# Splitting the gates' biases in the first layer, and running the last feed by halves of its tokens

## The chip, the core and the metric

The kernel runs on one core of a Trainium2 chip, in one launch. The time is the device time of an execution in microseconds. Measured times come from several executions; the profile comes from one execution of its own.

## What is computed

The reference is a chain of twelve blocks on 16 batches of 64 tokens with 256 features (1024 tokens), each added to its input after a layer norm. The change lies in four of them, one after the other:

```python
x = x + L0_xattn(layernorm(x), ctx_1024, ...)   # cross-attention, 16 heads, to 1601 context rows a batch
x = x + L0_attn(layernorm(x), ...)              # four encoder layers of linear attention, feed of 1024
x = x + L0_ffn(layernorm(x), ...)               # 8 experts, 2 for a token
x = x + L1_xattn(layernorm(x), ctx_1024, ...)   # slots: three rounds of attention and a GRU

# an encoder layer of L0_attn ends with
h = _layernorm(x, ln2_s, ln2_b)
h = jax.nn.relu(h @ W1 + b1) @ W2 + b2
return x + h
# the routing of L0_ffn
logits = x @ gate_w.T
top2_w, top2_idx = jax.lax.top_k(softmax(logits), 2)
counts = bincount(top2_idx); keep = counts <= cap
# the gates of L1_xattn
gx = x @ wih.T + bih
gh = h @ whh.T + bhh
r = sigmoid(xr + hr); z = sigmoid(xz + hz); n = tanh(xn + r * hn)
```

## The kernel before

A `Sections` object writes one method per block. `self.x` holds all tokens in on-chip memory as 8 tiles of 128 tokens (two batches each). The framework orders the instructions of each engine by their place in the program and by when it expects them to be ready, except where the code pins them (`keep_in_program_order`, the wrapper `Written`, the helpers `mm` and `tr`). So a load stands early in SP's queue when its memory is free, and blocks the loads behind it while it waits.

**First layer (`l0_xattn`).** `stream` walks the 16 batches' context in pairs of chunks. `load(b)` issues the two DMAs of batch b's transposed context `cT`; `maxima`, `weights`, `values` and `finish` work on one large score tile of PSUM ("w", one buffer). VectorE reduces maxima, ScalarE takes the exponential, POOL sums the weights into `tot` (tag "tot", two buffers). Products are pinned once the prologue is over, VectorE's instructions are not.

**Linear attention (`l0_attn`).** The tokens are in two halves `a` and `b` of 512, each with two pairs p of tiles. Small generators (`project`, `attend`, `feed`, `route`) yield between groups of instructions, and `go(it, n)` advances one by n steps, so that the order of all engines in this block is written by hand. `feed` turns the normed tokens, makes eight chunks c of 128 features of `relu(h @ W1 + b1)` over all 512 tokens (`by_feature`, 512 columns, evacuated by ScalarE for even c and by VectorE for odd), then four products with W2 (`by_token`, t) that VectorE adds to `y`; `measure` and `norm` are the two halves of a layer norm, `finish` the last one of the block. `squares` puts pieces of the slots' context norms on ScalarE in between. `route(s, p)` chooses the two experts of a pair's 256 tokens: turn, product with the gate (`gate`), a sort on VectorE (`rk_gt`, `rk_eq`, `rank`, `sel`), counts, the product `pos` (place of each token within its expert), the places on VectorE, and four indirect DMAs by POOL that scatter rows into the DRAM buffer `taken`. Counts run on from pair to pair, so routes come in order. The buffers of the routes lie in the pool "l0r", opened at the head of `l0_attn`; the rest is in pools on the right side of memory. PSUM's tag "mm" (chunks, `gate`, `pos`) has three buffers.

In the last layer, `a` ends first. Its two pairs are routed between the chunks of `b`'s feed, `b`'s two pairs after that feed.

**Experts (`l0_ffn`).** `xs` is read from `taken` once all scatters have landed, two products per expert follow, and results go to the DRAM buffer `given`.

**Slots (`l1_xattn`).** `load_keys` loads `cT` for the two batches of a tile (four DMAs of 832 KB), `load_rows` their rows `cn`. `product` multiplies weight matrices (`pw`). `biases` adds the two GRU biases, splits the sum in three BF16 parts on rows 24 to 26 of `bias`, which one product with `three` adds to the gates. `fetch(t)` gathers the experts' rows into `got`, `combine(t)` adds them to `self.x`, and from that `first` makes tile t's slots. `attend` (scores, turn, exponential) and `update` (`pu`, gates) follow by turns for two tiles at a time.

Of the kernel before, what the change touches and what calls it, by code (L numbers as in the profile page):

```python
# [64 lines left out]
class Sections:  # L65
# [135 lines left out]
    def l0_xattn(self):  # L201
        nc, tc, d = self.nc, self.tc, self.d
        with ExitStack() as ctx:
# [31 lines left out]
            def load(b):  # L235
                x = Streamed(b)
# [172 lines left out]
    def l0_attn(self):  # L409
# [3 lines left out]
        self.routed = ExitStack()  # L413
        pool = self.routed.enter_context(tc.tile_pool(name="l0r", bufs=1, reuse_waits="tile"))
        self.routes = to = Streamed(0)
# [18 lines left out]
        with ExitStack() as ctx:  # L434
# [260 lines left out]

            def route(s, p):
# [27 lines left out]
                V.tensor_tensor(to.count[:, 2 * g + 1], to.count[:, 2 * g], sel[:, 0], ALU.add)  # L724
                pos = ps.tile([P, 2, E], F32, tag="mm", name="pos", bufs=3, padded_shape=[P, 64, E])
# [89 lines left out]
            fb = feed(b, w, True)  # L815
# [3 lines left out]
            for p in range(2):  # L819
                measure(a, a.x, p)  # L820
                rt = route(a, p)
                go(fb, 1)
                norm(a, a.x, p)
                for _ in range(3):
                    go(rt, 1)
                    go(fb, 1)

            go(fb, 2)
            measure(b, b.x, 0)
            go(fb, 1)  # L830
            r0, r1 = route(b, 0), route(b, 1)
            norm(b, b.x, 0)
            go(r0, 1)
# [3 lines left out]
            go(r0, 1)  # L837
            go(r1, 1)
            go(r0)
            go(r1)  # L840
# [125 lines left out]

    def l1_xattn(self):
# [3 lines left out]
        with ExitStack() as ctx:  # L971
# [47 lines left out]

            at = ROWS_AT["L1_xattn_gru_bih"][0], ROWS_AT["L1_xattn_gru_bhh"][0]  # L1020
            raw, raw2 = (sb2.tile([32, 4 * D], F32, tag="e", name="raw", padded_shape=[32, NCH * P]) for _ in range(2))
            nc.gpsimd.memset(raw, 0.0)
            nc.gpsimd.memset(raw2, 0.0)
            for t, to, of, n in ((raw, 0, at[0], G), (raw, G, at[1] + 2 * D, D), (raw2, 0, at[1], 2 * D)):
                nc.sync.dma_start(t[24:27, to : to + n], d["rows"][:, of : of + n].to_broadcast([3, n]))
# [15 lines left out]

            bias = sb.tile([P, 4 * D], BF16, tag="bias", name="bias")
            three = sb.tile([P, P], BF16, tag="three", name="three")

            def biases():

                third = self.c("third")
# [1745 lines left out]
```

## Time and profile before

| | us |
|---|---|
| measured, 3 executions: median (lowest to highest) | 3773.07 (3768.23 to 3774.36) |
| the profiled execution: its time | 3775.53 |
| its span, first to last instruction | 3773.7 |
| first layer, to its last product | 0 to 863.9 |
| linear attention, to the landing of the last scatter | to 1356.5 |
| experts, to their last product | to 1383.7 |
| slots | to about 1930 |

The mean granted clock of TensorE is 0.957 of full speed. PE is TensorE, PEld its weight loads, DVE VectorE, ACT ScalarE, POOL GpSimd, SP SyncE; "q" behind an engine is its queue. A timeline line gives start, duration, engine, source line, operation, output<-input with shapes, a count, and in brackets how long the engine was idle before it and what ended the wait. L59 and L2429 are the lines of helpers, so groups are told apart by the names of tiles. A line by windows gives start:end and length, the busy time of PE, PEld, DVE, ACT and POOL with the number of instructions, then TensorE's granted clock, the busy share of the DMA engines and GB/s.

### The profile page before, as it was taken

What the parts mean: (1) busy time and instruction counts of PE and PEld (TensorE: products, weight loads), DVE (VectorE), ACT (ScalarE), POOL (GpSimd) and SP (SyncE); (2) the same over time, 40 slices, a digit from 0 to 9 for tenths busy, and PEclk for the clock granted to TensorE, in tenths of its full rate; (3) what the DMA queues carried; (4) which work ended last, traced back from release to release, by engine and by line L of the source; (5) the groups of instructions that cost most, each with busy time, mean ns of one, the idle gap of its engine ahead of it and who ended that gap; (6) DMA issues with size and microseconds to landing.
All of it is one profiled execution on the core that took longest, in us unless ns stands there. A gap on an engine that the chain in (4) does not pass through costs nothing.

```text
span 3773.7 us, 70724 instructions
## 1 busy us (share of the span) xinstructions
PE 3435.9 (91%) x30919; PEld 2176.2 (58%) x30934; DVE 1972.4 (52%) x3672; ACT 1450.6 (38%) x2072; POOL 1291.7 (34%) x789
## 2 busy tenths in 40 slices
PE   8999999996999858999977988999999789999986
PEld 4555555563666544555544666667767555555454
DVE  4344333345555546656656545576767655333346
ACT  2333333342444413444423443466666612111214
POOL 1555555561101132333321001577777630000012
PEclk9999999998999978999988999999999979999997
DMA  3111101101333352442101000211111004111650
GB/s 126 38 38 38 38 20 38 38 10 58 104 97 97 110 180 102 145 146 105 42 26 40 1 6 28 83 56 38 54 40 38 11 2 173 39 37 32 256 199 13
DMA packets 106046, 258.42 MB, mean 68 GB/s; under 512 B 9181, under 2 KB 74464, under 8 KB 103433
## 3 DMA queue, kind: packets, MB, share of 16 engines
q1 hardware_dynamic: 97288, 222.43, 16.6%
q10 hardware_dynamic: 6912, 27.27, 2.3%
q8 instruction: 243, 3.98, 0.4%
q0 software_dynamic: 1536, 4.20, 0.4%
q14 instruction: 67, 0.54, 0.0%
HBM read 248.10 MB, written 5.77 MB: 67 GB/s over the span
## 4 chain that ended last, share of the span: by engine, by line
PE 77%; DVE 12%; ACT 7%; issue 3%; POOL 0%; DMA 0%; ACTq 0%; SPq 0%; DVEq 0%; POOLq 0%
PE sc L2429 15%; PE pk L2429 15%; PE lin L2429 7%; PE acc L2429 6%; PE lin_t L2429 5%; ACT e L322 4%; PE pu L2429 4%; PE lin L194 3%; PE gate L1994 3%; PE up L1994 3%; PE pc L1616 3%; PE prz L2429 2%; PE gelu_t L1526 2%; PE turn L2434 2%; PE pn L2429 1%
## 5 line engine op out<-in xcount | busy, mean ns | idle before, releaser
L2362 POOL TENSOR_TENSOR tot<-tot,e 128x1024 f32<-128x1024 f32 (+1 forms) x340 | 803.3, 2363 | 374.6 <-ACT e L322 251.9
L265 DVE TENSOR_REDUCE m<-sc 128x4 f32<-128x2048 f32 x96 | 220.1, 2293 | 273.1 <-PE sc L2429 272.1
L1756 DVE SCALAR_TENSOR_TENSOR e<-sc,row_L_xattn_nbias,free 128x2048 f32<-128x2048 f32 x104 | 244.3, 2349 | 122.6 <-PE sc L2429 118.8
L1758 ACT ACTIVATE e<-e 128x2048 f32<-128x2048 f32 x104 | 198.7, 1910 | 243.0 <-DVE e L1756 243.0
L322 ACT ACTIVATE e<-sc 128x2048 f32<-128x2048 f32 x104 | 195.2, 1877 | 242.8 <-PE sc L2429 238.7
L2429 PE MATMUL sc<-qb,kT 32*128 32x128 f32 x6656 | 245.9, 284 | 36.3 <-DVE m L279 12.4
L2429 PEld LDWEIGHTS sc<-qb,kT 32*128 32x128 f32 x6656 | 207.0, 187 | 80.4 <-issue 24.5
L2429 PE MATMUL acc<-e,v 128*32 128x128 f32 x6656 | 226.3, 276 | 6.4 <-ACT e L1759 6.4
L2429 PEld LDWEIGHTS acc<-e,v 128*32 128x32 f32 x6656 | 170.0, 110 | 105.8 <-issue 95.2
L2429 PE MATMUL pk<-cT,wk 128*128 128x512 f32 (+1 forms) x512 | 207.5, 534 | 3.6 <-DVE rows L295 3.6
L2429 PE MATMUL pk<-wv,cT 128*128 128x256 f32 x832 | 208.6, 393 | 0.0
L1759 ACT ACTIVATE e<-e 128x2048 f32<-128x2048 f32 x104 | 198.7, 1911 | 3.3
L2429 PE MATMUL pk<-cT,wkv 128*128 128x512 f32 (+1 forms) x512 | 196.4, 524 | 0.0
L2429 PE MATMUL pk<-wkv,cT 128*128 128x256 f32 x832 | 196.3, 386 | 0.0
L2429 PEld LDWEIGHTS pk<-wv,cT 128*128 128x128 f32 x832 | 149.3, 189 | 75.2 <-issue 57.2
L2429 PEld LDWEIGHTS pk<-wkv,cT 128*128 128x128 f32 x832 | 153.2, 190 | 28.4 <-issue 4.3
L2429 PE MATMUL pu<-cn,e 128*64 128x257 f32 (+1 forms) x1248 | 146.6, 392 | 12.9 <-POOL e L1162 12.9
L1616 PE MATMUL pc<-ew,eh 128*128 128x256 f32 x640 | 155.0, 384 | 0.0
L1998 ACT ACTIVATE g<-gate 128x512 f32<-128x512 f32 x68 | 40.6, 597 | 292.2 <-PE gate L1994 292.2
L2429 PE MATMUL sc<-kT,qb 32*128 32x512 f32 (+2 forms) x1536 | 139.6, 463 | 11.4 <-ACT e L322 0.4
L1152 POOL TENSOR_TENSOR e<-e,mx 128x512 f32<-128x512 f32 x96 | 81.8, 884 | 195.2 <-DVE mx L1151 190.8
L2429 PE MATMUL sc<-cT,qT 128*64 128x512 f32 (+1 forms) x768 | 140.3, 518 | 0.5 <-DVE qT L1110 0.5
(521 smaller groups left out, 6229.2 us busy)
## 6 DMA issues: line engine op xcount, KB each, us to landing
cT<-in_ctx_t SPq DMA_DIRECT2D x128, 832.0 KB
cn<-in_ctx_n SPq DMA_DIRECT2D x32, 1664.0 KB
piece<-in_ctx_n ACTq DMA_DIRECT2D x32, 640.0 KB
w<-in_L_attn_W SPq DMA_DIRECT2D x8, 1024.0 KB
piece<-in_ctx_n ACTq DMA_DIRECT2D x16, 384.0 KB
w<-in_L_ffn_W SPq DMA_DIRECT2D x16, 256.0 KB
down<-in_L_ffn_w_down SPq DMA_DIRECT2D x16, 256.0 KB
gate<-in_L_ffn_w_gate SPq DMA_DIRECT2D x16, 256.0 KB
```

The costliest lines, as they stand in the source:

```text
L194: nc.tensor.matmul(pm, xT[:, k, t * P : (t + 1) * P], w[:, k, :], start=(k == 0), stop=(k == kc - 1))
L265: nc.vector.tensor_reduce(x.m4[:, g, :, i], pm, AX.X, ALU.max)
L322: nc.scalar.activation(e, pm, AF.Exp, scale=0.25)
L1152: pin(nc.gpsimd.tensor_tensor(p.e, p.e, p.mx.unsqueeze(2).to_broadcast(p.shape), ALU.subtract))
L1526: nc.tensor.matmul(pm, w[:, c, lo : lo + m], cT[:, c, :], start=(c == 0), stop=(c == nk - 1))
L1616: nc.tensor.matmul(pc[:, n, j, :], s.eh[i][:, c, tok], ew2[:, c, cols], start=False, stop=(c == 3))
L1756: nc.vector.scalar_tensor_tensor(e16, pm16, nb, free[:, at : at + P].unsqueeze(1).to_broadcast([P, 16, P]), ALU.add, ALU.mult)
L1758: nc.scalar.activation(e, e, AF.Relu)
L1759: nc.scalar.activation(e, e, AF.Square)
L1994: nc.tensor.matmul(pm[-1], w[:, k, n * P : (n + 1) * P], xT[:, k, tok], start=(k == 0), stop=(k == KC - 1))
L2362: nc.gpsimd.tensor_tensor(tot[:w], x.first if c == 1 else tot[:w], e[:w], ALU.add)
L2429: ins = self.nc.tensor.matmul(*args, **kw)
```

## The change

The biases of the slots' gates are laid out on the host as two arrays of 32 rows with zeros around the three used. They are loaded, added and split in `gate_biases`, which `load(1)` of the first layer calls; scratch is the buffers of "tot" and a new tag "part". The pool "l0r" is opened at the head of the first layer, holds `bias` and `three` besides the routes' buffers, and is closed behind the slots. In the last feed of `b`, `feed_last` takes the place of `feed`: 256 tokens at a time, so that the first pair is finished before the second's products. Pairs (a,0), (a,1) and (b,0) are routed among them, (b,1) behind. `route` has one more yield, between the sort and the product `pos`. The squares on ScalarE are spread otherwise: 18 in this feed instead of 26, the rest after the last route.

```diff
     def l0_xattn(self):
         nc, tc, d = self.nc, self.tc, self.d
+        self.held = ExitStack()
+        self.routed = self.held.enter_context(tc.tile_pool(name="l0r", bufs=1, reuse_waits="tile"))
...
             def load(b):
+                if b == 1:
+                    self.gate_biases(sb2)
...
     def l0_attn(self):
-        self.routed = ExitStack()
-        pool = self.routed.enter_context(tc.tile_pool(name="l0r", bufs=1, reuse_waits="tile"))
-        self.routes = to = Streamed(0)
+        pool, self.routes = self.routed, Streamed(0)
+        to = self.routes
...
+            def feed_last(s, w):
+                for p in range(2):
+                    turn(s, p, w.ln2_s, w.ln2_b)
+                    if p:
+                        add_row(s, w.b2)
+                    yield
+                for p in range(2):
+                    tok = slice(2 * p * P, (2 * p + 2) * P)
+                    for c in range(8):
+                        pm = ps.tile([P, 256], F32, tag="mm", name="lin_t", bufs=3, padded_shape=[P, 512])
+                        for k in range(KC):
+                            self.mm(pm, w.w1[:, k, c * P : (c + 1) * P], s.hT[:, k, tok], start=(k == 0), stop=(k == KC - 1))
+                        to, b1 = s.h1T[:, c, tok], w.b1[:, c : c + 1]
+                        if c % 2:
+                            V.tensor_scalar(to, pm, b1, 0.0, ALU.add, ALU.max)
+                        else:
+                            A.activation(to, pm, AF.Relu, bias=b1)
+                            squares(1)
+                        yield
+                    for t in range(2 * p, 2 * p + 2):
+                        pm = by_token(w.w2, t, s.h1T)
+                        squares(5 if p == 0 else 0)
+                        V.tensor_tensor(s.y[:, t, :], pm, s.y[:, t, :], ALU.add)
+                        yield
+                    measure(s, s.y, p)
+                    finish(s, p, True)
+                    yield
...
                 V.tensor_tensor(to.count[:, 2 * g + 1], to.count[:, 2 * g], sel[:, 0], ALU.add)
+                yield
                 pos = ps.tile([P, 2, E], F32, tag="mm", name="pos", bufs=3, padded_shape=[P, 64, E])
...
-            fb = feed(b, w, True)
+            fb = feed_last(b, w)
             go(fb, 2)
             go(fd)
             go(fb, 1)
-            for p in range(2):
-                measure(a, a.x, p)
-                rt = route(a, p)
+            for s, p in ((a, 0), (a, 1), (b, 0)):
+                rt = route(s, p)
+                measure(s, s.x, p)
                 go(fb, 1)
-                norm(a, a.x, p)
-                for _ in range(3):
+                norm(s, s.x, p)
+                for n in (1, 1, 1, 1):
+                    go(fb, n)
                     go(rt, 1)
-                    go(fb, 1)
-
-            go(fb, 2)
-            measure(b, b.x, 0)
-            go(fb, 1)
-            r0, r1 = route(b, 0), route(b, 1)
-            norm(b, b.x, 0)
-            go(r0, 1)
+                go(fb, 2)
             go(fb)
             measure(b, b.x, 1)
             norm(b, b.x, 1)
-            go(r0, 1)
-            go(r1, 1)
-            go(r0)
-            go(r1)
+            go(route(b, 1))
             squares(999)
...
+    def gate_biases(self, scratch):
+        nc = self.nc
+        raw, raw2 = (scratch.tile([32, 4 * D], F32, tag="tot", name="raw") for _ in range(2))
+        for j, to in enumerate((raw, raw2)):
+            nc.sync.dma_start(to, self.d["gate_bias"][j])
+        part = scratch.tile([32, 4 * D], BF16, tag="part", name="part", bufs=1)
+        bias = self.gate_bias = self.routed.tile([P, 4 * D], BF16, tag="bias", name="bias")
+        self.gate_rows = self.routed.tile([P, P], BF16, tag="three", name="three")
+        nc.gpsimd.memset(bias, 0.0)
+        third = self.c("third")
+        nc.vector.tensor_copy(self.gate_rows, third[:, 3:4].to_broadcast([P, P]))
+        nc.vector.tensor_tensor(raw, raw, raw2, ALU.add)
+        for j in range(3):
+            nc.vector.tensor_copy(part, raw)
+            nc.vector.tensor_tensor(raw, raw, part, ALU.subtract)
+            nc.vector.scalar_tensor_tensor(bias[:32], part, third[:32, j : j + 1], bias[:32], ALU.mult, ALU.add)
...
     def l1_xattn(self):
-            raw, raw2 = (sb2.tile([32, 4 * D], F32, tag="e", name="raw", padded_shape=[32, NCH * P]) for _ in range(2))
-            nc.gpsimd.memset(raw, 0.0)
-            nc.gpsimd.memset(raw2, 0.0)
-            for t, to, of, n in ((raw, 0, at[0], G), (raw, G, at[1] + 2 * D, D), (raw2, 0, at[1], 2 * D)):
-                nc.sync.dma_start(t[24:27, to : to + n], d["rows"][:, of : of + n].to_broadcast([3, n]))
...
-            bias = sb.tile([P, 4 * D], BF16, tag="bias", name="bias")
-            three = sb.tile([P, P], BF16, tag="three", name="three")
-            def biases():
...
+            bias, three = self.gate_bias, self.gate_rows
...
-            biases()
...
-            self.routed.close()
...
         self.pinned = False
+        self.held.close()
```

More of the change, by code (lines that the diff above doesn't have):

```diff
@@ L1018, in l1_xattn @@
             load_keys(tiles[0])
-            at = ROWS_AT["L1_xattn_gru_bih"][0], ROWS_AT["L1_xattn_gru_bhh"][0]
-            raw, raw2 = (sb2.tile([32, 4 * D], F32, tag="e", name="raw", padded_shape=[32, NCH * P]) for _ in range(2))
-            nc.gpsimd.memset(raw, 0.0)
-            nc.gpsimd.memset(raw2, 0.0)
-            for t, to, of, n in ((raw, 0, at[0], G), (raw, G, at[1] + 2 * D, D), (raw2, 0, at[1], 2 * D)):
-                nc.sync.dma_start(t[24:27, to : to + n], d["rows"][:, of : of + n].to_broadcast([3, n]))
             wv = self.w2(d["L1_xattn_Wv"], "wv")
@@ L1040, in first @@
                 self.layernorm_tile(sb2, self.x[:, s.t, :], s.s)
-            bias = sb.tile([P, 4 * D], BF16, tag="bias", name="bias")
-            three = sb.tile([P, P], BF16, tag="three", name="three")
-            def biases():
-                third = self.c("third")
-                nc.vector.tensor_copy(three, third[:, 3:4].to_broadcast([P, P]))
-                nc.vector.tensor_tensor(raw, raw, raw2, ALU.add)
-                part = sb2.tile([P, 512], F32, tag="scs", name="part", bufs=4)[:32].bitcast(BF16)
-                nc.gpsimd.memset(bias, 0.0)
-                for j in range(3):
-                    nc.vector.tensor_copy(part, raw)
-                    nc.vector.tensor_tensor(raw, raw, part, ALU.subtract)
-                    nc.vector.scalar_tensor_tensor(bias[:32], part, third[:32, j : j + 1], bias[:32], ALU.mult, ALU.add)
+            bias, three = self.gate_bias, self.gate_rows
             def product(out, w, r, by):
@@ L2753, in _lay_out @@
     out["rows"] = np.concatenate(rows)[None, :]
+    bi, bh = a["L1_xattn_gru_bih"], a["L1_xattn_gru_bhh"]
+    out["gate_bias"] = np.zeros((2, 32, 4 * D), np.float32)
+    out["gate_bias"][0, 24:27] = np.concatenate([bi, bh[2 * D :]])
+    out["gate_bias"][1, 24:27, : 2 * D] = bh[: 2 * D]
     vecs, at = [], 0
```

## The prediction

> **What bounds the kernel now.** I read the page's first sections, then the chain of waits from 1200 to 1500 us, then the timeline of that stretch, then DMA and clock by short windows. The page says that the whole is TensorE's:
>
> ```profile
> PE 3435.9 (91%) x30919; PEld 2176.2 (58%) x30934; DVE 1972.4 (52%) x3672; ACT 1450.6 (38%) x2072; POOL 1291.7 (34%) x789
> ...
> PE 77%; DVE 12%; ACT 7%; issue 3%; POOL 0%; DMA 0%; ACTq 0%; SPq 0%; DVEq 0%; POOLq 0%
> ```
>
> A change off TensorE therefore pays only where TensorE stands still. It touches two such places. The first is the start of the slots' attention (timeline):
>
> ```profile
> 1404.98 1.22 DVE L1049 TENSOR_TENSOR raw<-raw 32x1024 f32<-32x1024 f32 x1 [13.46 <-DMA raw<-in_rows]
> 1406.22 0.69 DVE L1053 CAST part<-raw 32x1024 bf16<-32x1024 f32 x1
> 1406.95 1.21 DVE L1054 TENSOR_TENSOR raw<-raw,part 32x1024 f32<-32x1024 f32 x1
> 1408.09 1.26 DVE L1055 SCALAR_TENSOR_TENSOR bias<-part,cst,bias 32x1024 bf16<-32x1024 bf16 x1
> ...
> 1415.63 0.98 DVE L1015 SCALAR_TENSOR_TENSOR x<-got,wt,x 128x256 f32<-128x256 f32 x2
> ...
> 1418.42 0.69 PE L2434 MATMUL turn<-cst,s 128*128 128x128 f32 x2 [27.43 <-DVE s L2297]
> ...
> 1422.23 6.63 PE L2429 MATMUL sc<-cT,qT 128*64 128x512 f32 x32 [0.52 <-DVE qT L1110]
> ```
>
> TensorE idles 27.43 us. VectorE waits 13.46 us for 18 KB of bias rows, splits them until 1415.6, and only then may add the experts' rows (combine(0)) from which the first slots come.
>
> The second place is the last feed and the routes. There TensorE waits for VectorE's chains, and its clock falls (timeline, then windows of 2 us, where 0.50 is the granted clock):
>
> ```profile
> 1292.08 0.78 PE L2434 MATMUL tr<-cst,n 128*128 128x128 f32 x4 [2.79 <-DVE n L59]
> ...
> 1297.35 0.40 PE L2429 MATMUL pos<-sel,places 128*128 128x16 f32 x2 [1.98 <-DVE sel L59]
> ...
> 1340.87 0.61 PE L2429 MATMUL pos<-sel,places 128*128 128x16 f32 x2 [6.07 <-DVE sel L59]
> ...
> 1350.12 1.03 POOL L751 DMA_INDIRECT taken<-n,put  x1 [1.79 <-DVE sm_mx L374]
> ```
> ```profile
> 1312.00:1314.00 2.00, 2.00 (x6) 1.48 (x7) 0.18 (x2) 1.69 (x9) 0.00 (x0) 0.50 0.96 308
> 1314.00:1316.00 2.00, 2.00 (x3) 0.72 (x3) 0.00 (x0) 1.22 (x7) 0.00 (x0) 0.50 0.40 140
> ```
>
> **The biases' removal from the slots.** Gone from VectorE: one add (1.22), three times cast, subtract and accumulate (0.69 + 1.21 + 1.27), a 0.22 cast for the rows: 10.9 us, and the wait before them. POOL loses three fills of 0.97 that ran beside a scatter's landing, SP three small DMAs. What is late next? Three candidates for combine(0) and the first scores:
> - The gathered rows. The windows of the software queue q0 give 0.12 MB from 1392 to 1395 and 0.36 MB from 1395 to 1398:
>
> ```profile
> q0 software_dynamic: 41, 0.12, 13.2%
> ...
> q0 software_dynamic: 126, 0.36, 31.9%
> ```
>
>  Tile 0 needs two gathers of 128 rows of 1 KB, 0.26 MB: moved by about 1396.2. With up to 1.8 us for completion (the trace gives 2.4 us from a scatter's issue to its landing, copying included) combine(0) starts near 1398. From it to the scores the chain takes 1422.23 - 1415.63 = 6.6 us (add, layer norm, turn, queries): 1404.6.
> - The context cT of tile 0, 3.4 MB, in the same SP queue ahead of the bias rows. Those landed at 1404.98, so it is there by about 1405.0. This is the later one.
> - The rows cn0 for the first update. After cT0, q1 moves about 0.2 MB a us; 3.4 MB from 1402 end near 1417.6, landed by 1419.4. The update began at 1438.92 and would now begin at 1421.7: 2 us of margin.
>
> So the first scores start at 1405.0, not 1422.23: **-17.2 us**. The ends: -18.2 if cT0 was there a microsecond before the rows behind it, -13 if cn0 or the fourth gather (q0 is busy until about 1418) comes a few us late. All later combines and loads shift along; the second tile's scores had 26 us of slack behind their cT.
>
> **The same work in the first layer.** `gate_biases` is called in load(1). It issues two DMAs of 128 KB on SP ahead of cT(1), 0.7 us at the 350 GB/s seen above; the second batch's first product is near 50 us, so nothing waits. POOL's fill falls into its idle first 20.9 us. `raw` and `raw2` take both buffers of "tot", so POOL's first sum (68.59) waits for the chain's end. VectorE gets the 10.9 us. In the prologue it stands idle 3.41, 2.80 and 7.28 us, and then between maxima:
>
> ```profile
> 17.68 0.69 DVE L124 COPY qT<-lin_t 128x512 f32<-128x512 f32 x1 [3.41 <-PE lin_t L181]
> 21.18 0.69 DVE L124 COPY qT<-lin_t 128x512 f32<-128x512 f32 x1 [2.80 <-PE lin_t L181]
> 29.14 0.42 DVE L263 SCALAR_TENSOR_TENSOR z<-sc,cst 128x256 bf16<-128x256 f32 x1 [7.28 <-PE sc L2429]
> 33.84 2.29 DVE L265 TENSOR_REDUCE m<-sc 128x4 f32<-128x2048 f32 x1 [1.49 <-PE sc L2429]
> 38.58 2.29 DVE L265 TENSOR_REDUCE m<-sc 128x4 f32<-128x2048 f32 x1 [2.44 <-PE sc L2429]
> ```
>
> That is 13.5 us before the first maxima, and 1.5 to 2.4 us in each period after. These instructions aren't pinned, so where they stand is not known. Behind the first of them, waiting for `raw`, would queue the copies of qT and the maxima, for which TensorE's next scores wait (one score tile). Ends: 0, and 10.9 if all lies on the path. I take **+0.5**, near the cover.
>
> **The pool opened earlier.** Before, SP stood 39.0 us at the load of wg (L420) until the first layer's last product at 863.95, because the pool lay on its memory; then wg, places and 1280 KB of zeros went ahead of the layer's bias rows. POOL waited for those rows until 873.57, and its two adds up to 879.3 held VectorE's `n` (877.06, 2.43 us). With the pool open from the start those loads no longer stand there; the rows can land 3 us sooner, but POOL's add needs VectorE's `n` of 872.9, so 1.7 us at most. **-1.0**, from -2 to +1 (another layout may hold a tile until 864).
>
> **The last feed and its routes.** I walk the written order with rows of before: a half chunk of the first product 0.86 (512 columns 1.72; the 256-column products of W2 run at 13.83 for 64, 0.216 each, so halving costs no column time), measure 1.37, norm 0.95, logits to `pos` 1.94, place 1.40, evacuation 0.5.
> - (a,0): the turn waits for `n` at 1291.86, after three half chunks (1288.2): idle 3.7 (before 2.8). The new yield puts a half chunk between sort and `pos`: 1.94 - 0.86, idle 1.2 with its releases (before 1.98).
> - (a,1): t0 and t1 (3.45 each) cover the turn (before 1.55). But b's measure and finish now stand ahead of the sort on VectorE: 4.1 + 1.94 after t1, against turn, copy, gate and a half chunk, 2.9: idle 3.3 (before 1.98).
> - (b,0): turn 1.15, `pos` 1.15. New.
>
> Idle 10.5 instead of 8.3, and the third route's own products (0.69 + 0.81 + 0.71 = 2.2) now in the stream: the last product ends 4.4 us later, at equal clock. Behind it: the wait for the last scatter falls from 1350.12 - 1331.2 = 18.9 to 15.1, since r0's norm and sort (0.84 and the wait until 1340.85) no longer stand before r1: r1's turn comes 6.75 after the last product, and from turn to scatter it is 1350.12 - 1341.74 = 8.4. So -3.8.
>
> **The clock, and a rule.** Before, the clock was 0.50 from 1297.6 to 1301 and from 1311.3 to 1318.3: half of 3.4 + 7.0, 5.2 us lost, after waits of 2 us and the tiny gate products. [...] I keep 5.2 (from 0 to 10): 4.4 - 3.8 = **+0.6**, from -5 to +5.5. ScalarE does 8 of the 26 squares after the routes, 8 x 0.40, while the scatter lands. W1's slot frees 11 us later, so SP's load of whh and the 4 MB queued behind it end near 1340; the experts read them after 1362.
>
> **Sum.** -17.2 + 0.5 - 1.0 + 0.6 = -17.1. The profiled execution had a span of 3773.7 and took 3775.53; with the change 3758.4. That execution stood 2.5 over the median of 3773.07; against the median it is **3756.0 us**. A difference of 0.2% is 7.5 us, about what a measurement here can tell from none.
>
> **Rivals.**
> - The loads take over (0.15): cn0, or the gathers, land 6 us or more late and half of the gain becomes a DMA wait. For it: 16 DMA engines over 95% busy from 1392 to 1436. Against: the byte count above. 3762 to 3766.
> - The split is exposed in the first layer (0.06): `raw` lands after 29 us and VectorE blocks in order; up to +10.9: -6, 3767, no measurable difference.
> - The tail gains as well (0.08): no half clock in the feed, -5 instead of +0.6: 3750 or less.
> - Slower (0.05): the clock stays at half from the first route to the last product. Some 30 us of products take 30 more, against 5.2 now: with the terms above 3756 + 25 = 3781. For it: five waits in 46 us where there were four in 47. Against: full clock came back within 7 us both times. It decides once more than 22 us are lost.
> - The split isn't off the path because the gate's rows still wait for something (0.03): same time.
>
> The likeliest case (0.63) spans 3750.5 to 3761. Range for 8 in 10: 3749.5 to 3765.5, to the DMA rival. Faster by over 0.2%: 0.63 + 0.08 + 0.15 and a part of the second rival, 0.88; same 0.07; slower 0.05.
>
> **What would show it.** TensorE's wait before the slots' first turn: about 10 us for 27.4; scores 14 us after the last `pw`, released by a cT DMA or the queries. The `raw` rows between 17 and 60 us, the first score tile's times unmoved. The last `lin` some 15 us before the last scatters, three routes ahead of it, two or more rows at 0.50. Wrong if the wait before the turn stays above 15, if `pu` waits for cn, or if VectorE's `z` at 29 us comes more than 3 us late.

## The result, and the profile after

The changed kernel takes 3752.96 us (median of 5 executions, 3749.33 to 3755.27) against 3774.36 for the kernel before beside it (5 executions, 3768.23 to 3781.62): a ratio of 0.9942, 95% interval 0.9927 to 0.9956. On another chip it came to 0.9931 (0.9914 to 0.9947). It was predicted at 3756.0 in 3749.5 to 3765.5. The profiled execution took 3753.96, with a span of 3752.2 and a mean granted clock of 0.959.

The total is right. To see whether its reasons are, I cut the spans at five marks that all these kernels share. Lengths in us; the last column is the changed kernel on the other chip:

| from, to | before | after | after, again |
|---|---|---|---|
| start, to the last addition but one to `y` of half `a`'s last feed (the expectations below call it the third layer's last) | 1280.65 | 1282.50 | 1281.29 |
| then to the experts' first load of `xs` (last feed, routes, scatter) | 75.89 | 78.94 | 79.20 |
| then to the slots' first scores (experts, first slots) | 65.70 | 47.55 | 46.44 |
| then to the first `lin_t` of the next attention, `l1_attn` (slots) | 518.54 | 518.26 | 518.01 |
| then to the end (not touched by the change) | 1833.0 | 1824.9 | 1824.55 |

Three things stand out. The third row alone gains 18.2. The second loses 3.1. And 8 us more are won in stages whose code is the same in both kernels; the prediction had nothing there. Up to the end of the slots the two profiles of the changed kernel are 13.5 and 15.8 us ahead of the one of before; the sum predicted 17.1.

On the page of the changed kernel, the busy time (with the share of the span and the instructions) and the chain's shares hardly differ from before:

```profile
PE 3440.3 (92%) x30966; PEld 2187.8 (58%) x30966; DVE 1974.1 (53%) x3676; ACT 1451.3 (39%) x2076; POOL 1291.0 (34%) x787
...
PE 77%; DVE 12%; ACT 7%; issue 2%; DMA 1%; POOL 1%; SPq 0%; ACTq 0%; DVEq 0%; POOLq 0%
```

TensorE has no less to do; it waits less. The timeline of the slots' start (the place of `raw`, `part` and the 27.43 us wait before):

```profile
1401.74 0.48 DVE L1059 SCALAR_TENSOR_TENSOR x<-got,wt,x 128x256 f32<-128x256 f32 x1 [4.39 <-DMA got<-given,get]
1402.88 0.48 DVE L1059 SCALAR_TENSOR_TENSOR x<-got,wt,x 128x256 f32<-128x256 f32 x1 [0.65 <-DMA got<-given,get]
...
1405.17 0.69 PE L2457 MATMUL turn<-cst,s 128*128 128x128 f32 x2 [8.34 <-DVE s L2320]
...
1408.99 6.38 PE L2452 MATMUL sc<-cT,qT 128*64 128x512 f32 x32 [0.52 <-DVE qT L1134]
...
1425.43 8.75 PE L2452 MATMUL pu<-cn,e 128*64 128x257 f32 x52 [7.30 <-POOL e L1186]
```

The first slots now wait for the gathered rows, 4.39 us, and not for the bias rows and their split. TensorE's wait is 8.34 instead of 27.43, and `pu` is released by POOL's `e`, not by the rows `cn`.

The first layer took the split in before its first maxima, in one row (timeline):

```profile
21.68 1.20 DVE L1005 TENSOR_TENSOR raw<-raw 32x1024 f32<-32x1024 f32 x1
...
32.06 1.27 DVE L1009 SCALAR_TENSOR_TENSOR bias<-part,cst,bias 32x1024 bf16<-32x1024 bf16 x1
33.26 0.41 DVE L268 SCALAR_TENSOR_TENSOR z<-sc,cst 128x256 bf16<-128x256 f32 x1
```

`z`, VectorE's first step of a batch, came at 29.14 before. It is 4.1 us late, more than the 3 us that the prediction allowed. In the last feed, TensorE's turns and the products `pos` wait as follows (timeline). The clock (0.50 or 1.00, the third figure from the right in the windows) is at half for longer:

```profile
1293.67 0.95 PE L2457 MATMUL tr<-cst,n 128*128 128x128 f32 x4 [3.65 <-DVE n L59]
...
1299.80 0.61 PE L2452 MATMUL pos<-sel,places 128*128 128x16 f32 x2
...
1318.49 0.61 PE L2452 MATMUL pos<-sel,places 128*128 128x16 f32 x2 [2.89 <-DVE sel L59]
...
1332.31 0.37 PE L2452 MATMUL pos<-sel,places 128*128 128x16 f32 x2 [1.10 <-DVE sel L59]
...
1346.68 1.22 PE L2457 MATMUL tr<-cst,n 128*128 128x128 f32 x4 [6.77 <-DVE n L59]
...
1355.12 0.96 POOL L785 DMA_INDIRECT taken<-n,put  x1 [11.93 <-DVE sm_mx L379]
```
```profile
1294.14:1304.38 10.24, 10.17 (x32) 8.18 (x31) 4.00 (x19) 1.45 (x4) 0.00 (x0) 0.50 0.00 0
1304.38:1318.04 13.66, 10.32 (x53) 8.66 (x51) 8.42 (x29) 6.93 (x29) 4.09 (x4) 1.00 0.50 166
1318.04:1324.87 6.83, 6.38 (x17) 5.30 (x18) 2.36 (x14) 0.87 (x3) 1.10 (x2) 0.50 0.00 0
```

Half clock lasts 10.24 + 6.83 = 17.07 us between the first route's turn and the feed's last product. Before, it was 3.42 + 6.83 = 10.25; the first line below is the window ahead of a fall:

```profile
1294.22:1297.63 3.41, 1.43 (x11) 1.14 (x10) 2.02 (x10) 1.99 (x7) 0.00 (x0) 1.00 0.21 29
1297.63:1301.05 3.42, 3.42 (x8) 1.87 (x8) 0.07 (x1) 0.00 (x0) 0.00 (x0) 0.50 0.44 166
...
1311.28:1318.11 6.83, 6.28 (x13) 3.85 (x14) 2.32 (x11) 3.52 (x18) 0.00 (x0) 0.50 0.58 163
```

### The profile page after: what moved, and what is told of

It is laid out like the page before. It is cut to its first block, busy times and chain, and to the rows that moved or that the text cites. A ratio compares the mean times of both kernels' runs of the same rounds, so it can differ in the third digit from the quotient of the medians.

```text
span 3752.2 us, 70803 instructions
## 1 busy us (share of the span) xinstructions
PE 3440.3 (92%) x30966; PEld 2187.8 (58%) x30966; DVE 1974.1 (53%) x3676; ACT 1451.3 (39%) x2076; POOL 1291.0 (34%) x787
## 4 chain that ended last, share of the span: by engine, by line
PE 77%; DVE 12%; ACT 7%; issue 2%; DMA 1%; POOL 1%; SPq 0%; ACTq 0%; DVEq 0%; POOLq 0%
PE sc L2452 15%; PE pk L2452 15%; PE lin L2452 7%; PE acc L2452 6%; PE lin_t L2452 5%; ACT e L327 5%; PE pu L2452 4%; PE lin L194 3%; PE gate L2017 3%; PE up L2017 3%; PE pc L1639 3%; PE prz L2452 2%; PE gelu_t L1549 2%; PE turn L2457 2%; PE pa L2452 1%
## 5 line engine op out<-in xcount | busy, mean ns | idle before, releaser
L2452 PE MATMUL sc<-qb,kT 32*128 32x128 f32 x6656 | 244.8, 283 | 36.6 <-DVE m L284 12.3
L2452 PE MATMUL sc<-kT,qb 32*128 32x512 f32 (+2 forms) x1536 | 140.8, 465 | 14.9 <-DVE m L270 2.3
L2022 DVE TENSOR_TENSOR hT<-up,g 128x512 f32<-128x512 f32 x68 | 47.0, 692 | 178.8 <-PE up L2017 174.6
```

Of the source, the lines that this page charges most:

```text
L2452: ins = self.nc.tensor.matmul(*args, **kw)
```

## The experiments

My theory after this reading: all of the gain up to the slots' end is the biases' removal; the new feed costs 3 us; the split costs some us in the first layer; and the 8 us behind the slots are the clock, not the change. The rivals: the feed gains too; the split is free; a load (cn0 or the gathers) now sets the slots' start; the later gain belongs to the change. A time of the whole program turned out to be a blunt tool here, as stages behind the change differ by more than most edits do, so each run is read by its stages as well. All ratios are to the kernel before on the same chip.

### One part alone

The biases alone: the changed kernel with the old last feed, the old order of routes and no new yield.

```diff
-            fb = feed_last(b, w)
+            fb = feed(b, w, True)
...
-            for s, p in ((a, 0), (a, 1), (b, 0)):
+            for p in range(2):
```

> The changed kernel with the old last feed and the old order of the routes (no extra yield); the biases' split in the first layer and the pool opened early stay. Measured in the profile as the stretch from the experts' first load of xs to the slots' first score product (65.7 us before, 47.6 with the whole change). Theory of parts: the biases alone make that stretch 47.6 within 1.5 us, the stretch from the last addition of the third layer's feed to the load of xs is the old 75.9 within 1.5, and the time is 17 to 20 us under the kernel before (3754 to 3757 for 3774). Rival, that the earlier third route made part of that gain: the stretch stays over 50 us and the time is 12 us or less under before.

The feed alone: the kernel before with `feed_last`, the new routes and the yield.

```diff
-            fb = feed(b, w, True)
+            fb = feed_last(b, w)
...
                 V.tensor_tensor(to.count[:, 2 * g + 1], to.count[:, 2 * g], sel[:, 0], ALU.add)
+                yield
```

> The kernel before with the new last feed and route order alone; biases, their load and the pool as before. Theory of parts: from the last addition of the third layer's feed to the load of xs 75.9 before becomes 78.9 within 2 us, as with the whole change (its last product 7 us later, the tail behind it 4 us shorter); the stretch from xs to the first scores stays 65.7 within 1.5; the time is 0 to 5 us above before. Rival, that the rerouting is a gain which the profile of the whole change hid behind one more window at half clock: if the half-clock windows in this stretch number two instead of five, the stretch is 74 or less and the time is below before by 2 us or more.

| | median (lowest to highest), executions | ratio | last feed to `xs` | `xs` to scores | slots' end at | from there to the end |
|---|---|---|---|---|---|---|
| biases alone | 3764.06 (3756.67 to 3770.81), 16 | 0.996 (0.995 to 0.997) | 75.93 | 47.96 | 1925.88 | 1843.15 |
| feed alone | 3776.92 (3763.19 to 3781.56), 20 | 0.9998 (0.9988 to 1.0007) | 78.84 | 65.05 | 1939.40 | 1822.0 |

The feed alone makes no difference that can be measured, and its stage is 3 us longer. So it is in all profiles: 78.8 to 79.2 us in the ten with the new feed and its yield, 75.9 in the three with the old, with the same 17.07 and 10.24 us at half clock. The biases alone bring the 17.7 us of the third stage. So the gain up to the slots' end is the biases'.

The times do not add up so well. The biases alone are 11.8 us under before, where 17 to 20 were expected, and measure 11 us more than the whole change, although in their profile the slots end 1.4 us earlier. Their profiled execution (the slowest of the 16) loses 18 us behind the slots, in code that the edit doesn't touch; that of the feed alone, the fastest of its 20, gains 11 there. That is followed up at the end.

The biases alone also lost a part of their gain again. In their timeline the scores stop half way, which in the changed kernel ran on:

```profile
1406.06 4.84 PE L2430 MATMUL sc<-cT,qT 128*64 128x512 f32 x16 [0.52 <-issue]
...
1412.48 0.69 ACT L1134 ACTIVATE scs<-sc,sr 128x512 f32<-128x512 f32 x1 [4.46 <-remote]
1413.22 2.38 PE L2430 MATMUL sc<-cT,qT 128*64 128x512 f32 x16 [2.32 <-ACT scs L1134]
```

From the scores to the first `pu` it is 19.59 us, for 16.68 before and 16.44 and 17.84 in the two profiles of the changed kernel; the kernel with the split on GpSimd, below, shows the same wait and 20.31. What held ScalarE is not named by the trace ("remote"). The context's packets that the trace holds end at 1406.5, 6 us before ScalarE goes on; a late piece of the context is neither shown nor excluded.

### What the split costs, and where it can go

Only the rows early: the split goes back to its old place in the slots, but its rows are loaded ahead of cT of tile 0, so that VectorE needs no wait for them.

```diff
-                if b == 1:
-                    self.gate_biases(sb2)
...
+            for j, to in enumerate((raw, raw2)):
+                nc.sync.dma_start(to, d["gate_bias"][j])
...
+            biases()
```

> The changed kernel with the split back at its old place in the slots, but its rows loaded by two DMAs ahead of tile 0's context, so that VectorE has no rows to wait for; nothing of the split in the first layer. Theory one, the wait for the rows was the larger share and the gathers end at 1401.7 anyway: the split starts with the end of mvg's last eviction (1397.4 in the changed kernel), ends 10.9 us later, and the first scores come 6.6 us later than with the change: 54 us from xs to the first scores, the time 4 to 7 us over the changed kernel. Theory two, wait and work weigh alike because the rows' landing is bound by the shared engines and not by the queue's order: the split starts at 1401 or later, 58 us or more, 10 us over the changed kernel. In the first layer the scores of the second product come at 32.6 again, for 36.6, and the layer ends 0.4 to 1.4 us earlier.

Measured 3760.18 (3753.43 to 3762.31, 8 executions), ratio 0.995 (0.9935 to 0.9965). Its timeline at the slots' start:

```profile
1397.55 1.21 DVE L1069 TENSOR_TENSOR raw<-raw 32x1024 f32<-32x1024 f32 x1 [1.50 <-DMA raw<-in_gate_bias]
...
1406.98 1.27 DVE L1075 SCALAR_TENSOR_TENSOR bias<-part,cst,bias 32x1024 bf16<-32x1024 bf16 x1
1408.17 0.99 DVE L1039 SCALAR_TENSOR_TENSOR x<-got,wt,x 128x256 f32<-128x256 f32 x2
```

The split still stands ahead of the experts' rows: they are added 47.2 us after `xs`, against 59.1 before and 40.3 after. From `xs` to the scores it is 53.85. That is the 54 of theory one. So of the 18.2 us, about 12 were the wait for the rows (65.70 to 53.85) and 6 the split itself (53.85 to 47.55). VectorE's 10.9 us of work cost only 6, mostly because it began 3.7 us before the gathered rows are added in the changed kernel (36.6 us after `xs` for 40.3).

The split on GpSimd: the changed kernel with the same steps on POOL, in the first layer.

```diff
-            nc.vector.tensor_copy(part, raw)
-            nc.vector.tensor_tensor(raw, raw, part, ALU.subtract)
-            nc.vector.scalar_tensor_tensor(bias[:32], part, third[:32, j : j + 1], bias[:32], ALU.mult, ALU.add)
+            nc.gpsimd.tensor_copy(part, raw)
+            nc.gpsimd.tensor_tensor(raw, raw, part, ALU.subtract)
+            nc.gpsimd.tensor_scalar(part, part, third[:32, j : j + 1], None, ALU.mult)
+            nc.gpsimd.tensor_tensor(bias[:32], bias[:32], part, ALU.add)
```

> The changed kernel with the split's fifteen instructions on GpSimd in place of VectorE, which is idle from 26 to 71 us of the span. Estimate: 13 of about 2.4 us (its 128x1024 addition takes 2.35), 31 us, ending near 60. Theory one, the split on VectorE costs little by the end of the first layer since TensorE works on: the second score product is back at 32.6, but the layer ends only 0.4 to 1.4 us earlier, and the time is that of the changed kernel within its noise. Theory two, the four us at the start are lost in full and something else brought them back later in the layer: the layer ends 3 to 4 us earlier than the changed kernel's. Against both, if GpSimd's chain runs past 71 us the first sum of a batch waits and the layer ends later than the changed kernel's.

The split twice: VectorE's three steps are done six times, the last three on a rest that is zero.

```diff
-        for j in range(3):
+        for j in (0, 1, 2, 0, 1, 2):
```

> The changed kernel with the three steps of the split run twice (the second time on the rest, which is zero): nine more instructions on VectorE in the first layer's start, 9.6 us. With one split the maxima come 4.1 us late and the layer ends some 2 us late, at equal clock. Theory one, half of what VectorE delays there is regained within the layer: it ends 4 to 6 us later than the changed kernel's. Theory two, only the idle time of the first batches, once 2 us, can be regained: it ends 8 to 10 us later. Theory three, the scheduler puts the added steps between the maxima, where VectorE idles 1.5 to 3.3 us each time: under 2 us later.

Medians: 3760.78 (3746.61 to 3762.33, 8), ratio 0.9949 (0.9931 to 0.9967) on GpSimd; 3757.52 (3749.77 to 3762.71, 4), ratio 0.9956 (0.9941 to 0.9971) twice. Neither can be told from the changed kernel by its time. The first layer can, from its first query product to its last `xT`, set beside the us at half clock in it:

| | first layer | at half clock |
|---|---|---|
| no split there: feed alone / before / rows early | 844.50 / 847.65 / 848.06 | 0 / 7.6 / 7.5 |
| split on VectorE: after / again | 849.17 / 849.18 | 3.4 / 3.4 |
| split twice on VectorE | 851.98 | 4.1 |
| split on GpSimd | 844.92 | 0 |

If a us at half clock costs half a us, 847.65 at 7.6 is 843.8 at none, within 0.7 of the 844.50 of the feed alone. At that rate the split on VectorE costs 849.17 - 844.50 - 1.7 = 3.0 us, and on GpSimd 0.4. The seven profiles with one split on VectorE come to 846.1 to 847.5 at full clock, so it costs 1.6 to 3.6 us, by which of the kernels without it one takes. On GpSimd `z` is back at 29.66, and the chain ends long before the first sum (timeline):

```profile
23.61 2.34 POOL L1005 TENSOR_TENSOR raw<-raw 32x1024 f32<-32x1024 f32 x1
29.66 0.42 DVE L268 SCALAR_TENSOR_TENSOR z<-sc,cst 128x256 bf16<-128x256 f32 x1 [7.28 <-PE sc L2453]
...
49.58 2.11 POOL L1010 TENSOR_TENSOR bias<-bias,part 32x1024 bf16<-32x1024 bf16 x1
67.55 2.35 POOL L2386 TENSOR_TENSOR tot<-e 128x1024 f32<-128x1024 f32 x1 [15.86 <-ACT e L327]
```

Done twice, the 9.6 us more cost about 2.5 (851.98 at 4.1 against 849.17 at 3.4), nearest to theory three: in that timeline the added steps stand between the maxima. So the stage pays for a part of VectorE's time only. The first split stuck out of its gap: the idle times of 3.4 and 2.8 us before it stayed empty, and its 11.6 us in a row stood in the 7.28 us before `z`.

### Whether a load stands behind the gain

The rows of `cn` for tile 0 are held back: a one-column copy into `cn`, ordered on VectorE behind the experts' addition, stands before its DMA.

```diff
+                    if s is tiles[0]:
+                        tc.keep_in_program_order(nc.vector.tensor_copy(cn[:, 0, :1], self.x[:, 0, :1]))
```

> The changed kernel; VectorE writes one element of each of the two buffers of tile 0's rows cn0 behind its second combine, so that SP's two loads of cn0 (3.4 MB) can't be issued before, and tile 1's first context chunk goes ahead of them. Theory one, the bytes of cn0 share the engines with the gathers and with tile 0's context and so set the first scores: combine(0), 40.3 us after the load of xs in the changed kernel, comes 2 to 4 us earlier, the first scores 2 to 4 us earlier (44 to 46 us after xs, for 47.6). Theory two, the queue serves in order and cn0 stands behind the context anyway: combine(0) and the first scores stay within 0.7 us. In both, cn0 is issued near 46 us after xs instead of 34, and needs some 9 us at the 0.38 MB a us seen here: at 57 to 61 us, when the first pu was due at 64 after xs; if it lands later, pu waits for DMA cn and the gain is lost (time the changed kernel's or up to 5 us over it).

Measured 3763.51 (3750.72 to 3770.29, 6), ratio 0.9951 (0.9932 to 0.997). The scores come 46.95 us after `xs` (47.55 and 46.44 without the hold), and the last piece of cT of tile 0 lands 48.3 us after `xs`, as it does without (48.1). That is theory two. `cn` lands only at 1427.5, and `pu` comes 17.63 behind the scores, which the changed kernel without the hold did too (16.44 and 17.84). So holding the later load back does not make the earlier one faster. In the two profiles of the changed kernel the cT lands 48.1 and 46.6 us after `xs` and the scores start at 47.55 and 46.44: cT and the chain from the gathered rows end together. To start the scores sooner, both would have to come sooner.

### The clock

The feed's new yield is left out:

```diff
                 V.tensor_tensor(to.count[:, 2 * g + 1], to.count[:, 2 * g], sel[:, 0], ALU.add)
-                yield
```

> The changed kernel without the new yield between the sort and its products of positions, so that pos follows the gate products directly. By the prediction's own step (TensorE waits 1.98 us for the sort without a half chunk in between, 1.2 with it) three routes wait 2.3 us more: from the third layer's last addition to the feed's last 56.1 us for 53.8. By the clock, if a wait of 2 us starts another half-clock window, more: 57.5 to 59.5. Against both, if the waits for the turn absorb it: 53.8 within 0.5.

Measured 3762.86 (3759.42 to 3772.28, 10), ratio 0.9967 (0.9957 to 0.9978). The stage grows from 78.94 to 82.61, and `pos` waits longer:

```profile
1319.56 0.61 PE L2451 MATMUL pos<-sel,places 128*128 128x16 f32 x2 [3.98 <-DVE sel L59]
...
1334.19 0.40 PE L2451 MATMUL pos<-sel,places 128*128 128x16 f32 x2 [1.97 <-DVE sel L59]
```

20.5 us of the feed are at half clock instead of 17.1. The yield is worth 3.7 us, more than the 2.3 of the waits alone, as the clock's theory had it: without it the change's feed would cost twice as much.

Then I put products that nobody reads into TensorE's waits, to see whether its clock then stays up. First into the wait for the last scatter:

```diff
+                pm = ps.tile([P, D], F32, tag=tag, name="fill", bufs=3, padded_shape=[P, 512])
+                for k in range(n):
+                    self.mm(pm, ws[0][0][:, 0, :P], ws[0][1][:, 0, :], start=(k == 0), stop=(k == n - 1))
...
+            fill(28, "out")
```

> The changed kernel with 28 products of 128x256 (weights of expert 0 with themselves, into a PSUM tile that nobody reads) on TensorE while it waits 10.8 us for the scatters and the load of xs. Theory one, the half clock behind that wait costs time on the path: with the clock full again by 1364, the stretch of the experts from xs to the first pw (28.0 us in the changed kernel, 8 of them at half clock) takes 25 to 26.5. Theory two, VectorE's and ScalarE's evictions set the pace of the experts: no more than 0.7 us. If the fillers at half clock run longer than the wait (28 of 0.43 would be 12 us), xs's turn starts late by up to 2 us.

Or into the two waits of the slots' start, ahead of the turn (28 products) and ahead of the first `pu` (24):

```diff
+            fill(28, "sc")
...
+            fill(24, "sc")
```

> The changed kernel with 28 such products (weights wv and wih) behind the weights' products in the slots, where TensorE waits 8.3 us, and 24 more before the first pu, where it waits 7.3 us. Theory one, the half-clock windows behind these two waits are on the path: pq takes 1.1 us instead of 2.1, and the first 52 products of pu 5.9 instead of 8.7; from the first scores to the third tile's weights the path is 3 to 4.5 us shorter. Theory two, the context of tile 0 lands at 48 us after xs whatever TensorE does (it landed 0.6 us after the first score product began): nothing before the scores, and at pu 2.8 at most. If a filler runs past the wait it costs what it overlaps, under 1 us.

| | median (lowest to highest), executions | ratio | `xs` to first `pw` (experts) | `xs` to scores |
|---|---|---|---|---|
| filler in the scatter | 3759.51 (3756.23 to 3762.94), 4 | 0.994 (0.9919 to 0.996) | 27.26 | 47.06 |
| fillers in the slots | 3764.33 (3756.05 to 3773.22), 6 | 0.9957 (0.9938 to 0.9977) | not touched | 49.31 |

Both fillers were too long (timelines; the records hold two for each product):

```profile
1353.46 14.34 PE L2459 MATMUL fill<-w,w 128*128 128x256 f32 x56
```
```profile
1396.84 12.35 PE L2460 MATMUL fill<-wih,wv 128*128 128x256 f32 x56
```

They cover waits of 10.8 and 8.3 us, so the turns behind them started 3 to 4 us late. The 24 products ahead of `pu` took 10.53 us, 0.44 each; of the first filler, the first six records (three products) took 2.91 us, 0.97 a product. In the profiles of before and after, records of 128x256 start 0.216 us apart (median) where the granted clock is 1.00 and 0.427 apart where it is 0.50. The first filler's experts then took 3.2 to 3.9 us less from their late turn on and ended where they did without it (27.99 and 27.23 us after `xs` in the two profiles of the changed kernel): the clock's gain and the overrun cancelled.

So the fillers were cut to 18, 17 and 15 products, together with the split on GpSimd:

```diff
+            fill(18, "out")
...
+            fill(17, "sc")
...
+            fill(15, "sc")
```

> The changed kernel with the split on GpSimd and with filler products cut to the length of the waits: a filler of 128x256 took 0.44 us at full clock and 0.88 at half in the two runs before, so 18 while the scatters land, 17 before tile 0's turn and 15 before the first pu. Theory one, the half clock behind each wait is on the path: from xs to the first pw 24.5 us (28.0 in the changed kernel, 27.3 with a filler that ran 3.3 us over), from the first scores to the weights of tile 3 some 3 us less, and the first layer about 2 us shorter: 7 to 9 us under the changed kernel at the same pattern of the later stages. Theory two, tile 0's context lands at 48 us after xs whatever TensorE does, so what the experts gain is lost before the scores: 3 to 5 us.

And the same with the old feed and the old order of routes, which by their stages would be the best of the parts:

```diff
-            fb = feed_last(b, w)
+            fb = feed(b, w, True)
```

> The same with the old last feed and the old order of the routes. From the third layer's last addition to the load of xs 75.9 us in place of 78.9 to 79.2. Theory one, stages add: 3 us under the kernel with GpSimd's split and fillers and the new feed, 10 to 12 under the changed kernel at the same pattern of the later stages. Theory two, whatever comes early waits for tile 0's context (from the first scores to the first pu 19 to 20 us, as in two kernels that came there 3 to 5 us earlier than the changed one): no gain from the old feed.

| | median (lowest to highest), executions | ratio | `xs` to first `pw` | `xs` to scores | slots' end at | from there to the end |
|---|---|---|---|---|---|---|
| new feed | 3751.74 (3743.76 to 3762.61), 6 | 0.994 (0.9924 to 0.9956) | 24.82 | 43.66 | 1920.00 | 1827.1 |
| old feed | 3753.2 (3750.26 to 3757.09), 5 | 0.994 (0.9927 to 0.9952) | 24.91 | 43.57 | 1914.52 | 1838.9 |

In the timeline of the one with the new feed the filler ends about a us before the rows land, and the experts run at full clock throughout (windows of it, then of the changed kernel, over the experts):

```profile
1350.47 10.19 PE L2468 MATMUL fill<-w,w 128*128 128x256 f32 x36
1361.68 0.63 PE L2473 MATMUL tr<-cst,xs 128*128 128x128 f32 x4 [1.02 <-DMA xs<-taken]
...
1421.06 5.87 PE L2468 MATMUL pu<-cn,e 128*64 128x257 f32 x50 [1.18 <-DMA cn<-in_ctx_n]
```
```profile
1361.60:1383.40 21.80, 20.89 (x150) 17.79 (x150) 9.79 (x26) 6.30 (x14) 0.00 (x0) 1.00 0.39 125
```
```profile
1364.20:1389.40 25.20, 24.32 (x150) 20.92 (x150) 9.79 (x26) 6.29 (x14) 0.00 (x0) 0.83 0.35 112
```

150 records of products at a granted clock of 1.00 take 21.80 us, at 0.83 they take 25.20. Up to the slots' end the two kernels are 7.3 and 12.7 us ahead of the first profile of the changed kernel, 4.9 and 10.4 of the second: the stages add, as both first theories had it. With the new feed `pu` now waits for `cn`, so the loads are next in line. In the medians nothing of all this can be seen; the totals that were expected, 7 to 12 us under the changed kernel, did not come.

### The stages behind the change

The changed kernel was run once more, unchanged, on the chip of the hold and of the first fillers.

> The changed kernel once more. In the profiles so far the code behind the slots, the same in all kernels, took from the first product of the next attention to the end 1833 us in the kernel before, 1825 with the change, and 1843, 1822, 1828 and 1835 in four other kernels, and the half-clock windows in it moved likewise. Theory one, the 8 us that this stretch was shorter with the change are where the windows fell in one execution: this profile gives 1828 or more, and the median over more runs is nearer to 17 than to 21 us below before. Theory two, the shift makes the later stages faster in every execution: 1823 to 1827 again, and 20 us or more.

Measured 3752.84 (3751.08 to 3760.16, 6), ratio 0.9931 (0.9914 to 0.9947), 24.7 us below before, and again 1824.55 us from the slots' end. That is theory two. Over the 14 profiles of this study that last stretch takes 1819 to 1843 us in the same code. One piece of it, the attention `l2_attn` from its first product `pk` (values with keys) to the first product with `wg` of the block behind it, has just three lengths:

| length | at half clock | profiles |
|---|---|---|
| 71.2 | 14.9 | after, again, feed alone, split twice, GpSimd split with fillers |
| 75.8 | 26.5 | before, and the six others |
| 79.3 | 32.9 | biases alone, old feed with GpSimd split and fillers |

In the profiles of before and after the granted clock is 1.00 or 0.50, and each of the 132 stretches at one value between its first change and its last is a whole number of windows of 3.41 us. Where the first `pk` lies behind the border of such a window separates the three: 1.65 to 1.75 us behind it the piece takes 71.2, from 1.76 to 1.93 it takes 75.8, at 1.36 to 1.37 it takes 79.3. This was found afterwards, in 14 profiles, and no run set the phase on purpose; it was 1.88 us in the profile of before and 1.65 in that of after. The windows of before and after at one of these falls:

```profile
3089.59:3099.83 10.24, 10.24 (x128) 7.73 (x122) 3.36 (x7) 1.88 (x1) 10.16 (x2) 0.50 0.01 2
3099.83:3123.72 23.89, 20.10 (x455) 16.71 (x454) 22.40 (x39) 0.00 (x0) 0.31 (x2) 1.00 0.01 3
```
```profile
3086.14:3089.55 3.41, 2.85 (x78) 2.62 (x67) 3.38 (x4) 0.00 (x0) 0.00 (x0) 1.00 0.02 5
3089.55:3092.96 3.41, 3.41 (x56) 2.44 (x58) 2.64 (x7) 0.00 (x0) 0.00 (x0) 0.50 0.00 0
3092.96:3103.20 10.24, 7.08 (x148) 5.36 (x140) 8.28 (x16) 0.00 (x0) 0.00 (x0) 1.00 0.01 2
```

Before, three windows in a row are at half; after, one. This piece gives 4.6 of the 8.1 us that the changed kernel wins behind the slots.

Another 4.1 lie in the first 59 us behind the mark: up to VectorE's 46th instruction there, before takes 58.65 us and the two profiles of the changed kernel 54.51 and 54.35. Before, TensorE stands 1.93 us for nothing that the trace shows ("issue"), and two windows at half clock follow; after, the same products run on (timeline and windows of before, then the timeline of after):

```profile
1989.56 0.21 PE L2429 MATMUL acc<-eT,ones 64*32 64x64 f32 x1 [1.93 <-issue]
```
```profile
1987.15:1990.57 3.42, 1.49 (x56) 1.01 (x38) 0.76 (x1) 0.00 (x0) 0.00 (x0) 1.00 0.64 193
1990.57:1997.39 6.82, 6.75 (x171) 5.54 (x170) 4.31 (x6) 2.23 (x3) 0.00 (x0) 0.50 0.03 5
```
```profile
1973.07 0.91 PE L2452 MATMUL acc<-eT,ones 64*32 64x64 f32 x64
```

The rest of the stretch gives nothing in sum. It is no shorter work: behind the mark VectorE, ScalarE and GpSimd have the same 1543, 681 and 293 instructions in all 14 profiles. That it is the clock alone is not shown: the whole stretch has 187.7 us at half clock before and 179.7 after (165.7 in the second profile), which at half a us each is 4.0 of the 8.1. Why the changed kernel fell into the short pattern in both of its profiles is open; of its 11 timed executions 8 lie below 3755, so it is not one lucky profile.

## Why the prediction was right

**The biases' removal, -17.2.** Right in size and in reason: 18.2 us less from `xs` to the scores in the first profile, 19.3 in the second, 17.7 with the biases alone. The candidates were right too. The last piece of cT was put at 48.5 us after `xs` and landed at 48.1; the gathered rows were put at 41.5 and their additions came at 40.3 and 41.4; queries 48.1, scores at 47.55. The margin of `cn` was thin, as said: its second half lands 64.6 and 63.5 us after `xs`, and `pu` starts at 64.0 and 64.3; it is the next wait once the rest is faster (1.18 us with the split on GpSimd and fillers). Whether the 3 us that the biases alone lose between scores and `pu` are the rival's, in which the loads take over, is not shown.

**The split, +0.5.** A mis-sized term: it measured 1.6 to 3.6 us. The prediction set 10.9 us of work against 13.5 us of idle time in three gaps. But the ten instructions ended up in one row from 21.68 to 33.3, behind the first two gaps, and only the 7.28 us before `z` covered them. In the stage table only 1.9 us shows, as the profiled execution of before had one more window at half clock there.

**The pool, -1.0.** Not seen. From the first layer's last addition but one to `xT` to the first `lin` of wkv it is 32.4 to 32.6 us with the old pool and with the new, at the same 19 us of half clock, and 30.5 (old) against 31.4 to 31.6 (new) at 15 to 16: 0 to +1. The bias rows come earlier as predicted, but POOL's addition waits for VectorE (timeline, after):

```profile
868.72 1.09 POOL L59 TENSOR_SCALAR bk<-row_L_attn_bk.0_7275 128x256 f32<-128x256 f32 x1 [7.80 <-DMA row_L_attn_bk.0_7275<-in_rows]
...
873.68 2.50 POOL L59 TENSOR_TENSOR y<-y,row_L_attn_bk.0_7275 128x1024 f32<-128x1024 f32 x1 [3.87 <-DVE n L59]
```

**The feed, +0.6.** Its walk held: the waits were put at 3.7 (turn of (a,0)), 3.3 (sort of (a,1)), 1.15 (`pos` of (b,0)) and 6.75 (last turn), and measured 3.65, 2.89, 1.10 and 6.77; that of `pos` of (a,0), put at 1.2, did not occur, as the half chunk ahead of it ran at half clock and took 2.05 us. The products end 3.3 to 3.5 us later at equal clock for the 4.4 predicted, and the tail is 3.4 to 3.8 shorter for 3.8. The step that failed is the one that kept the loss by half clock at 5.2: it is 8.5, by two more windows. So the term is +2.9 to +3.3 in every kernel with the new feed and its yield.

**The clock's loss.** The falls in this feed followed windows in which TensorE was busy for 1.43 and 1.99 of 3.41 us before (from 1294.22 and 1307.87), and for 0.47 and 0.97 after (from 1290.73 and 1314.63). Of the 68 falls in the profiles of before and after, 11 followed a window without any product, and 63 one that was idle for 42% or more. Busy time does not decide alone: at 3089.59 above, before, TensorE is busy for 10.24 of 10.24 us and the clock stays at half. The products there are small (64x33 and 32x128 among them); what the clock counts, these runs don't show. Keeping the loss that before showed was right in sign, and still too mild, because it took the loss over instead of counting which windows the new waits would fall into. The narrower products of this feed cost nothing that can be seen: at equal clock the feed's later end is explained by the longer waits (9.5 us for 8.3) and the third route's own products (2.2, the prediction's figure).

**The sum.** -18.2 + 1.9 + 3.1 - 0.3 = -13.5 up to the slots' end (-15.8 in the second profile), for -17.1: the feed's clock and the split were too cheap. The total came out within about 3 us of the forecast because later stages gave 8 us that nothing in the prediction stood for. That part of the number was luck.

## What to carry to other kernels

When work is taken off a wait, list what is late next with its time after a mark that both kernels share: here a load and a chain ended within a microsecond of each other, so the gain was theirs to set. Before judging variants of a long program that differ by under 10 us, compare lengths of stages at equal clock; totals carry what happens to the stages behind the edit. Idle time of an engine covers a moved chain only where its instructions can be spread over the gaps, and here only in part (2.5 of the 9.6 us added were still paid); look for an engine that is idle in one piece, as GpSimd was here (45.01 us ahead of its first sum in the changed kernel).

## What was not expected of the hardware

In the profiles of before and after the clock changes only by whole windows of 3.41 us, and the same product falls elsewhere on their grid in each: the first `pk` of `l2_attn` stands 1.88 us behind a border before and 1.65 after. A window with 1.99 of 3.41 us of products was followed by one at half (before, from 1307.87), and windows that the trace shows full of small products stayed at half (before, 10.24 of 10.24 us from 3089.59). The attention `l2_attn`, the same code, took 71.2, 75.8 or 79.3 us, and the length went with where it started on that grid. Over the timed executions of the kernel before (chip by chip, 72 on three), 0.001 of mean granted clock stands for 1.7 to 2.3 us of its time. Fillers that fit their waits (18, 17 and 15 products) removed all half clock from `xs` to the scores (20.2 us in the changed kernel), and won 2.4 to 3.2 us in the experts; no total showed it.
